# A Macaron block with a selective scan: the scan's gate copies issued one background part behind their products, in pinned order, with the Silu behind the last

## The chip, the cores and the metric

The kernel runs on one core of one Trainium2 chip. The time is device microseconds of one execution; the kernel before was run three times, with a median of 3204.71 us. In the lines of the profile PE is TensorE (matmuls), PEld its weight loads, DVE is VectorE, ACT is ScalarE, POOL is GpSimd and SP is SyncE, which issues nearly all DMAs here. All data is fp32.

## The reference

The input x has 4 sequences of 1024 rows of 512 columns. The block is half an FFN, a selective-scan (Mamba) layer, and half an FFN again:

```python
def ffn(x):                      # INTER = 1408
    g = einsum('th,ih->ti', x, gate_w) * gate_s
    u = einsum('th,ih->ti', x, up_w) * up_s
    return einsum('ti,hi->th', silu(g) * u, down_w) * down_s

def attn(x):                     # I = 1024, N = 16, K = 4, R = 128
    proj = einsum('blh,oh->bol', x, W_in)
    h, gate = split(proj, 2)                       # 1024 channels each
    h = silu(depthwise_conv(h, conv_w) + conv_b)
    ts, Bm, Cm = rms of the three parts of einsum('bil,oi->blo', h, Wx)
    delta = softplus(einsum('blr,ir->bil', ts, Wdt) + dt_bias)
    # per channel and per state n, along l:
    #   s = exp(delta * A) * s + delta * Bm * h ;  y += s * Cm
    y = (scan + D * h) * silu(gate)
    return einsum('bil,hi->blh', y, Wout)

x = x + 0.5 * ffn(layernorm(x))
x = x + attn(layernorm(x))
x = x + 0.5 * ffn(layernorm(x))
```

The change is about the `gate` half of `proj` and its Silu.

## The kernel before

The 4096 rows are cut into 16 stages of 256 rows (`k` = 0 to 15, four for each sequence). A stage scans its 256 rows; beside the scan it works through a list of background parts. The scan of a stage is 8 groups `i` of 128 channels with 4 units `g` each. A unit (`unit`, lines 557 to 596) makes four exponentials on ACT (L573, PSUM tiles `da`), two products on POOL (L578, tiles `sb`), four scans on DVE (L582) and two products with C on DVE (L592). A unit's sums over the states are small matmuls on PE (`yps`, L604), issued four units at a time one unit behind. PSUM has four tiles for `da`, and three (`ps_m`, banks 5, 6 and 7) that every other product shares: FFN products, the scan's gate products, the convolution's, the transposes.

The background of stage k (`background`, L717) is a list of parts made by hand: the FFN of other rows (11 parts `gate_w`, each a product and an eviction on ACT, L287; 11 parts `up_w`, evicted by DVE, L304; then `down_w`), and woven between them, two to an FFN part, the 8 parts of the scan's own gate (`gate`, L538), the two transposes of the next stage's rows (`tpm`, evicted on ACT, L238), the output projection of the stage before (`op`, L637, added by DVE, L645) and the convolution of the next stage (`hp`, L376, first tap on ACT, L380, three taps on DVE, L387). In stages 1 to 15 the order is: `gate_w` 0, 1, 2, then gate parts 0 and 1, `gate_w` 3, gate parts 2 and 3, `gate_w` 4, gate parts 4 and 5, `gate_w` 5, gate parts 6 and 7, `gate_w` 6, the two transposes, `gate_w` 7, the first half of `op`, `gate_w` 8, the second half, and so on. After `gate_w` 3, 7 and 10 a Silu over the evicted columns follows (`silu`, L197); it loads a table before it and after it. The number of FFN rows beside a stage (`BESIDE`, L39) is 512 in stages 2, 3, 5, 6, 8, 9, 11 and 12, which are called wide here, and 384 in the others, called narrow. Stage 0 has `up_w` parts in place of `gate_w` parts.

A gate part is four matmuls into a `ps_m` tile (`gp`, L545) and a copy of 128x256 to the resident tile `g_all` (L549). After the eighth copy Silu runs over all of `g_all` (2048 columns). `gated` (L614) multiplies the scan's result by it on POOL, from group 4 of the same stage on.

The main loop (L795) emits a unit and then as many parts as their cost allows. Two things set the order on an engine. A scheduler orders what was emitted, and may move an instruction if nothing ties it. `pin` (`keep_in_program_order`) ties an instruction behind the one that was emitted on its engine directly before it. And `defer(parts, f)` (L154) holds a piece of emission back until so many further parts with a cost have been emitted (`passed`, L158); `do` (L168) emits the part first and then what has come due. Before the change the gate copy is emitted with its own product, and is pinned in stage 0 alone.

Of the kernel before, what the change touches and what calls it, by code (L numbers as in the profile page):

```python
# [20 lines left out]
NI = I // P  # L21
NF = INTER // P
T = 256
# [19 lines left out]
def macaron_kernel(ctx: ExitStack, tc: tile.TileContext, a: dict, out: bass.AP):  # L43
    nc = tc.nc
# [37 lines left out]
    g_all = const.tile([P, NI, T], F32, name="g")  # L82
# [68 lines left out]
    pin = tc.keep_in_program_order  # L151
    deferred = []

    def defer(parts, emit):  # L154

        deferred.append([parts, emit])
# [33 lines left out]
    def cols(t):  # L190
        return t.rearrange("p (k o) -> p k o", k=KH)
# [5 lines left out]
    def silu(t):  # L197

        pin(nc.scalar.activation(t, t, AF.Silu))
        pin(nc.scalar.preload_act_table_set("natural_log_exp_and_others"))  # L200
# [42 lines left out]
    class FFN:  # L243
# [35 lines left out]
        def gate(self):  # L279
            self.done = 0  # L280

            def part(it):
                def emit(w):
                    if it == 0:
                        self.hd = p1.tile([P, NF, 2 * T], F32, tag="hd", name=f"hd{self.name}")
                    gp = self.product("gate_w", it, w[0])
                    nc.scalar.activation(  # L287
                        self.hd[:, it, : self.n], gp, AF.Copy, scale=gate_s[:, it : it + 1]
                    )
                    if it % 4 == 3 or it == NF - 1:  # L290
                        h = self.hd[:, self.done : it + 1, : self.n]
                        silu(h)
                        self.done = it + 1

                return Work(KH * self.n, 0, emit, [("gate_w", it)], settled=it == 0)

            return [part(it) for it in range(NF)]
# [240 lines left out]
    def gate(k):  # L538
        def part(i):
            def emit(w):  # L540
                assert k == 0 or ("gated", i) in st[k - 1]
                gp = ps_m.tile([P, 512], F32, tag="mm", name=f"gp{k}_{i}")
                w = cols(w[0])
                for kk in range(KH):
                    nc.tensor.matmul(  # L545
                        gp[:, :T], lhsT=w[:, kk, :], rhs=st[k]["xnT"][:, kk, K - 1 :],
                        start=(kk == 0), stop=(kk == KH - 1),
                    )
                (nc.scalar.copy if k else lambda *t: pin(nc.scalar.copy(*t)))(g_all[:, i, :], gp[:, :T])  # L549
                if i == NI - 1:  # L550
                    silu(g_all)

            return Work(KH * T, 0, emit, [("W_in", NI + i)])

        return [part(i) for i in range(NI)]
# [363 lines left out]
```

## Time and profile before

| what | value |
|---|---|
| three runs | 3203.93 to 3205.31 us, median 3204.71 us |
| the profiled execution | 3208.17 us, of which its span is 3206.3 us |
| granted TensorE clock, mean | 0.986 |
| gate copies L549 | 128, 47.5 us busy, 371 ns each |
| matmuls of the gate parts L545 | 1024, 388 ns each |
| table loads on ACT, L199, L200 and L573 | 86, 86 and 2, 1283 ns each |
| Silu of `g_all` | 16, 1912 ns each |
| exponentials L573 | 2048, 472 ns each |

The span runs from the first instruction to the last. The durations below come from this one execution. Its time is 3.5 us above the median of the runs.

Each row of a timeline gives start, duration, engine, line, operation, out<-in, shape, how many were merged, and in brackets how long the engine sat idle before it and what ended that.

### The profile page before, as it was taken

The page shows a single profiled execution, that of the slowest core. Times are in us where ns is not written, and L with a number is a line of the kernel's source. Part 1 is how long each engine was busy: PE and PEld are TensorE (multiplying, and loading weights), DVE is VectorE, ACT ScalarE, POOL GpSimd, SP SyncE. Part 2 cuts the span into 40 slices and gives each one's busy share as a digit, 9 for nine tenths or more (in the row PEclk, how much of TensorE's full clock was granted, in tenths as well). Part 3 has the DMA queues.
Part 4 walks back from the last instruction along what each step waited for, and adds up shares of the span by engine and source line. Part 5 has one row for each costly group of instructions (what it writes and reads, how often), then busy time and mean ns, then how long its engine had stood idle before and what let it go on. Part 6 is the DMA issues. An engine that isn't in the chain of part 4 may idle for free.

```text
span 3206.3 us, 41927 instructions
## 1 busy us (share of the span) xinstructions
PE 3059.7 (95%) x12448; PEld 1644.7 (51%) x12448; DVE 2477.8 (77%) x4981; ACT 1780.1 (56%) x3531; POOL 1938.5 (60%) x1895
## 2 busy tenths in 40 slices
PE   8988899999999999999999999999999999899999
PEld 3554454545555454545545454554555455454434
DVE  1259788888869887887988788798878779798931
ACT  3265555747465664646565474656557475656530
POOL 0066758566766766666675756667575667658610
PEclk9999999999999999999999999999999999999999
DMA  5364566556566655645665654656565564566531
GB/s 171 113 174 119 158 188 171 161 137 184 134 174 181 178 161 148 184 123 160 191 178 159 164 164 123 183 165 171 168 178 161 140 186 132 170 183 178 169 94 43
DMA packets 287427, 506.43 MB, mean 158 GB/s; under 512 B 32097, under 2 KB 50273, under 8 KB 287201
## 3 DMA queue, kind: packets, MB, share of 16 engines
q1 hardware_dynamic: 285616, 503.31, 55.8%
q8 instruction: 100, 1.64, 0.2%
q14 instruction: 127, 1.03, 0.1%
q10 hardware_dynamic: 1584, 0.45, 0.1%
HBM read 442.03 MB, written 61.60 MB: 157 GB/s over the span
## 4 chain that ended last, share of the span: by engine, by line
PE 63%; DVE 21%; ACT 6%; POOL 5%; issue 5%; DMA 1%; DVEq 0%; SPq 0%; POOLq 0%; ACTq 0%
DVE da L582 12%; PE fo L319 12%; PE gate_w L273 12%; PE up_w L273 9%; PE hp L376 5%; PE op L637 5%; PE gp L545 5%; PE yps L604 5%; DVE sb L592 4%; POOL sb L578 3%; ACT da L573 2%; PE gate_wp L273 1%; PE gate_we L273 1%; PE dp L490 1%; PE foe L319 1%
## 5 line engine op out<-in xcount | busy, mean ns | idle before, releaser
L578 POOL TENSOR_TENSOR sb<-rep,bc 128x512 f32<-128x512 f32 x1024 | 1279.4, 1275 | 421.3 <-PE yps L604 302.8
L582 DVE TENSOR_TENSOR_SCAN da<-da,state,sb 128x256 f32<-128x256 f32 x1536 | 1059.7, 740 | 250.9 <-ACT da L573 215.6
L573 ACT ACTIVATE da<-rep,a_w 128x256 f32<-128x256 f32 x2048 | 899.5, 472 | 508.9 <-DVE sb L592 488.0
L592 DVE TENSOR_TENSOR sb<-da,bc 128x512 f32<-128x512 f32 x1024 | 688.8, 680 | 1.7 <-issue 0.4
L273 PE MATMUL gate_w<-fxT,w_gate_w 128*128 128x384 f32 (+1 forms) x1408 | 564.2, 547 | 8.6 <-ACT hd L287 6.3
L273 PE MATMUL up_w<-fxT,w_up_w 128*128 128x384 f32 (+1 forms) x1408 | 557.8, 546 | 3.0 <-DVE hd L304 2.4
L319 PE MATMUL fo<-w_down_w,hd 128*128 128x512 f32 x1232 | 549.4, 599 | 0.0
L273 PEld LDWEIGHTS gate_w<-fxT,w_gate_w 128*128 128x128 f32 x1408 | 268.1, 193 | 256.2 <-issue 154.9
L604 PE MATMUL yps<-sb,fold 128*32 128x256 f32 x4096 | 332.0, 389 | 62.8 <-DVE sb L592 54.1
L273 PEld LDWEIGHTS up_w<-fxT,w_up_w 128*128 128x128 f32 x1408 | 260.7, 190 | 254.1 <-issue 150.8
L582 DVE TENSOR_TENSOR_SCAN da<-da,sb 128x256 f32<-128x256 f32 x512 | 322.6, 679 | 78.6 <-ACT da L573 62.2
L319 PEld LDWEIGHTS fo<-w_down_w,hd 128*128 128x128 f32 x1232 | 230.1, 192 | 273.0 <-issue 271.5
L521 POOL TENSOR_SCALAR e<-z 128x512 f32<-128x512 f32 x64 | 124.4, 1944 | 237.3 <-ACT z L502 223.1
L604 PEld LDWEIGHTS yps<-sb,fold 128*32 128x32 f32 x4096 | 127.7, 110 | 271.4 <-DVE sb L592 122.9
L376 PE MATMUL hp<-mxT,w_W_in 128*128 128x259 f32 x1024 | 244.3, 386 | 23.1 <-issue 12.4
L545 PE MATMUL gp<-mxT,w_W_in 128*128 128x256 f32 x1024 | 244.7, 388 | 4.0 <-ACT dd L499 3.3
L376 PEld LDWEIGHTS hp<-mxT,w_W_in 128*128 128x128 f32 x1024 | 192.5, 191 | 83.5 <-issue 30.4
L637 PE MATMUL op<-w_Wout,u 128*128 128x512 f32 x512 | 228.1, 595 | 0.3 <-POOL u L616 0.3
L545 PEld LDWEIGHTS gp<-mxT,w_W_in 128*128 128x128 f32 x1024 | 195.4, 193 | 63.0 <-issue 19.8
L387 DVE SCALAR_TENSOR_TENSOR u<-hp,conv_w,u 128x256 f32<-128x256 f32 x384 | 178.0, 473 | 14.7 <-ACT u L380 12.2
L287 ACT ACTIVATE hd<-gate_w,gate_s 128x384 f32<-128x384 f32 (+1 forms) x176 | 110.5, 629 | 130.4 <-PE gate_w L273 129.6
L304 DVE SCALAR_TENSOR_TENSOR hd<-up_w,up_s,hd 128x384 f32<-128x384 f32 (+1 forms) x176 | 118.2, 672 | 69.0 <-PE up_w L273 68.9
(112 smaller groups left out, 2649.9 us busy)
## 6 DMA issues: line engine op xcount, KB each, us to landing
rep<-row SPq DMA_DIRECT2D x512, 256.0 KB, 4.9
w_W_in<-in_W_in_dram SPq DMA_DIRECT2D x256, 256.0 KB, 3.6
w_gate_w<-in_gate_w_dram SPq DMA_DIRECT2D x198, 256.0 KB, 4.0
w_up_w<-in_up_w_dram SPq DMA_DIRECT2D x198, 256.0 KB, 4.1
w_down_w<-down_w SPq DMA_DIRECT2D x187, 256.0 KB, 2.7
row<-dd SPq DMA_DIRECT2D x128, 256.0 KB, 3.4
w_Wout<-in_Wout_dram SPq DMA_DIRECT2D x128, 256.0 KB, 4.6
bc<-bcd SPq DMA_DIRECT2D x64, 256.0 KB, 4.9
```

The source lines that it names most:

```text
L273: nc.tensor.matmul(o[:, : self.n], lhsT=w[:, k, :], rhs=self.xT[:, k, : self.n], start=(k == 0), stop=(k == KH - 1),)
L319: nc.tensor.matmul(op, lhsT=self.hd[:, it, t * P : (t + 1) * P], rhs=wd[it], start=(it == 0), stop=(it == NF - 1),)
L376: nc.tensor.matmul(hp[:, : K - 1 + T], lhsT=w[:, kk, :], rhs=st[k]["xnT"][:, kk, :], start=(kk == 0), stop=(kk == KH - 1),)
L387: pin(nc.vector.scalar_tensor_tensor(u[:, i, :], hp[:, q : q + T], conv_w[:, i, q : q + 1], u[:, i, :], ALU.mult, ALU.add,))
L521: lambda: pin(nc.gpsimd.tensor_scalar(e, z, 1.0, 1.0, ALU.add, ALU.subtract)),
L545: nc.tensor.matmul(gp[:, :T], lhsT=w[:, kk, :], rhs=st[k]["xnT"][:, kk, K - 1 :], start=(kk == 0), stop=(kk == KH - 1),)
L573: e = nc.scalar.activation(da[:, j, :], rep[:, h + j, 0, :], AF.Exp, scale=a_w[:, b0 + h + j, g : g + 1])
L578: nc.gpsimd.tensor_tensor(sb, rep[:, hs, 1, :], d["bc"][:, g : g + 1, :].to_broadcast([P, 2, T]), ALU.mult)
L582: nc.vector.tensor_tensor_scan(da[:, j, :], da[:, j, :], sb[:, j, :], 0.0 if first else state[:, b0 + h + j, g : g + 1], ALU.mult, ALU.add,)
L592: nc.vector.tensor_tensor(sb, da, d["bc"][:, NS + g : NS + g + 1, :].to_broadcast([P, 2, T]), ALU.mult)
L604: nc.tensor.matmul(yp[j * Q : (j + 1) * Q, :], lhsT=fold, rhs=pr[j // 2][:, j % 2, :], start=(g == 0), stop=(g == NS - 1),)
L637: nc.tensor.matmul(op, lhsT=st[k]["u"][:, i, j * P : (j + 1) * P], rhs=wo[i], start=(i == 0), stop=(i == NI - 1),)
```

## The change

Product and copy of a gate part are separated. The copy is put off by one part with a cost, and every copy is pinned, in all stages. The Silu is emitted right behind the eighth copy, as before, so it is put off with it.

```diff
                         gp[:, :T], lhsT=w[:, kk, :], rhs=st[k]["xnT"][:, kk, K - 1 :],
                         start=(kk == 0), stop=(kk == KH - 1),
                     )
-                (nc.scalar.copy if k else lambda *t: pin(nc.scalar.copy(*t)))(g_all[:, i, :], gp[:, :T])
-                if i == NI - 1:
-                    silu(g_all)
+
+                def out_of():
+                    pin(nc.scalar.copy(g_all[:, i, :], gp[:, :T]))
+                    if i == NI - 1:
+                        silu(g_all)
+
+                defer(1, out_of)
 
             return Work(KH * T, 0, emit, [("W_in", NI + i)])
```

The functions that it calls:

```python
    def defer(parts, emit):
        deferred.append([parts, emit])

    def passed(entries):
        for e in entries:
            e[0] -= 1
        while deferred and deferred[0][0] <= 0:
            deferred.pop(0)[1]()

    def silu(t):
        pin(nc.scalar.activation(t, t, AF.Silu))
        pin(nc.scalar.preload_act_table_set("natural_log_exp_and_others"))
```

Built, the changed program has the same instructions as before on PE, DVE, POOL and SP, and one table load more on ACT. SP's order is the same throughout. On ACT, in a wide stage (stage 3), the part of the order that differs reads as follows (c0 to c7 are the gate copies, e3 is the eviction of `gate_w` 3, S a Silu with its two table loads, t0 and t1 the evictions of the two transposes, x4 four exponentials):

```
before  c0 c1 e3 S c2 x4 c3 x3 e4 x c4 x4 c5 x .. x2 e5 c6 c7 S(g) e6 t0 x8 e7 x S t1 x7
after   c0 e3 S c1 x4 c2 x3 e4 c3 x c4 x5 .. x2 e5 c5 c6 e6 c7 S(g) t0 x4 e7 x S t1 x8
```

In a narrow stage (stage 4):

```
before  c0 x2 c1 e3 S c2 c3 x5 e4 x3 c4 x3 c5 x .. e5 x c6 x3 c7 S(g) e6 t0 e7 S x4 t1 x8
after   c0 x2 e3 S c1 x4 c2 e4 c3 x4 c4 x4 .. e5 c5 x2 c6 x2 e6 c7 S(g) t0 e7 S x4 t1 x8
```

The three `ps_m` banks are also dealt out in another order. In stage 3, for example: `gate_w` 4 takes the bank of gate product 1 (before: that of `gate_w` 3), gate product 5 that of `gate_w` 4 (before: that of gate product 3), gate product 7 that of `gate_w` 5 (before: that of the `dp` product), the second transpose that of `gate_w` 6 (before: that of gate product 7), and `gate_w` 7 that of gate product 7 (before: that of `gate_w` 6).

## The prediction

> **What bounds the kernel now.** First the page's busy times and the chain of waits.
>
> ```profile
> PE 3059.7 (95%) x12448; PEld 1644.7 (51%) x12448; DVE 2477.8 (77%) x4981; ACT 1780.1 (56%) x3531; POOL 1938.5 (60%) x1895
> ...
> PE 63%; DVE 21%; ACT 6%; POOL 5%; issue 5%; DMA 1%; DVEq 0%; SPq 0%; POOLq 0%; ACTq 0%
> ```
>
> PE leads, with 146.6 us idle in all, and DVE holds a fifth of the chain. So any gain has to come out of those 146.6 us. Next, windows: length, then busy time of PE, PEld, DVE, ACT and POOL. The first is the gate part of stage 3 (wide), the last that of stage 4 (narrow).
>
> ```profile
> 732.50:765.80 33.30, 33.30 (x173) 21.47 (x171) 25.17 (x42) 26.40 (x47) 22.55 (x25) 1.00 0.77 217
> 800.50:860.00 59.50, 58.15 (x265) 30.98 (x265) 52.96 (x97) 30.40 (x68) 37.38 (x41) 1.00 0.51 136
> 916.20:951.20 35.00, 31.39 (x173) 21.54 (x171) 27.02 (x59) 26.53 (x49) 27.11 (x28) 1.00 0.74 209
> ```
>
> In a wide stage PE has no idle moment while the gate is computed: there is nothing to win there, and a PE wait that appears is lost. In a narrow stage PE idles 3.6 us. Third, the table of waits (total, times, longest):
>
> ```profile
> DVE da L582 <- ACT da L573: 277.8, 88, 11.2
> ACT g L549 <- PE gp L545: 49.5, 36, 5.2
> ```
>
> DVE starves when exponentials come late, and ACT spends 49.5 us standing at a gate copy whose product isn't ready, with exponentials queued behind. That is the most the change could take off ACT. Fourth, the timeline of ACT in stage 3 around Silu of `g_all`, and DVE beside it:
>
> ```profile
> 759.75 0.37 ACT L549 COPY g<-gp 128x256 f32<-128x256 f32 x1 [0.81 <-PE gp L545]
> 760.14 1.28 ACT L199 ACT_TABLE_LOAD   x1
> 761.43 1.91 ACT L199 ACTIVATE g<-g 128x2048 f32<-128x2048 f32 x1
> 763.36 1.28 ACT L200 ACT_TABLE_LOAD   x1
> 764.66 0.69 ACT L287 ACTIVATE hd<-gate_w,gate_s 128x512 f32<-128x512 f32 x1
> 765.24 0.58 ACT L238 COPY mxT<-tpm 128x512 f32<-128x512 f32 x1
> 765.71 3.27 ACT L573 ACTIVATE da<-rep,a_w 128x256 f32<-128x256 f32 x8
> ```
> ```profile
> 767.09 2.68 DVE L582 TENSOR_TENSOR_SCAN da<-da,state,sb 128x256 f32<-128x256 f32 x4 [4.06 <-ACT da L573]
> ...
> 776.46 0.76 DVE L582 TENSOR_TENSOR_SCAN da<-da,state,sb 128x256 f32<-128x256 f32 x1 [1.21 <-ACT da L573]
> ```
>
> The 4.5 us of the Silu with its two loads (760.14 to 764.64) run while PE makes `gate_w` 6 (759.55 to 762.98). That is the overlap the change touches.
>
> **The change part by part, wide stages (8).** I walk stage 3. (a) Copy 1 now stands behind eviction 3 and a Silu, and ends at 745.2, where copy 2 ended (744.81 + 0.37); `gate_w` 4 needs that bank and started at 744.91: PE waits 0.3. Gate product 5 now needs eviction 4, which ended at 751.37; PE is there at 750.4 (748.34 + 1.73 + 0.3): 1.0 more. The second transpose needs eviction 6, about 0.35 behind the first: PE is 1.7 late at `gate_w` 7. (b) Silu of `g_all` now starts behind eviction 6 and copy 7. `gate_w` 6 ends at 762.98 + 1.4 = 764.4; eviction 0.69, copy 0.37, Silu block 4.50 and transpose eviction 0.58 bring the next exponentials to 770.5 instead of 765.71: 4.8 us. Queued behind are t0 and x4, and DVE waits for the latter: its scans start at 771.9 instead of 767.09. (c) Then the Silu of `gate_w` 4 to 7 comes, and before it only 5 exponentials instead of 9 now stand. DVE works off its one unit in 4.0 us (to 775.9) and waits again: eviction 7, one exponential, the block and t1 end at 778.4, scans go on near 778.8. The unit that started at 776.46 starts one unit later, near 783: DVE is 6.5 late. (d) A DVE wait of 1.2 for `op` (at 786.72) takes 1.2 back: 5.3. (e) What PE feels of it:
>
> ```profile
> 802.52 0.76 DVE L582 TENSOR_TENSOR_SCAN da<-da,state,sb 128x256 f32<-128x256 f32 x1 [1.95 <-POOL sb L578]
> 803.74 0.76 DVE L582 TENSOR_TENSOR_SCAN da<-da,state,sb 128x256 f32<-128x256 f32 x1 [0.46 <-POOL sb L578]
> ```
> ```profile
> 796.89 3.67 PE L376 MATMUL hp<-mxT,w_W_in 128*128 128x259 f32 x16
> ```
>
> The first product's taps (L387, four groups of 0.46 to 1.65 us from 793.64) free a bank near 795.9, which convolution product 2 wants at 796.89: 1.0 of slack. In the changed order a scan and a product (1.4 us) move behind these taps. So PE starts that product 5.3 - 1.4 - 1.0 = 2.9 late. On DVE's side the waits of 1.95 and 0.46 for POOL swallow 2.4 of the 5.3, which leaves 2.9 as well. Behind this both engines are nearly full (58.15 and 52.96 of 59.5 us), so 2.9 stays. Stage 2 by the same steps: scans 580.46 to 585.25, 6.3 late at the third unit, no wait for `op`, slack 1.5, hence 3.4 on PE; POOL waits of 2.66 leave 3.6 on DVE: 3.5. Stages 5, 8, 11 look like 2, and 6, 9, 12 like 3. Sum: 4 x 3.5 + 4 x 2.9 = 25.6 us.
>
> A bound below: DVE's lateness hidden wholly, PE's own 1.65 a stage, 13 us. Above: none hidden, 4 x 6.3 + 4 x 5.3 = 46 us. I take 25.6, since each deduction has a row.
>
> The price of a table set. [...] Here the load row is 1.28 and Silu starts 0.01 behind its end. [...]
>
> **Narrow stages.** In stage 4:
>
> ```profile
> 927.10 0.37 ACT L549 COPY g<-gp 128x256 f32<-128x256 f32 x1
> 930.67 0.37 ACT L549 COPY g<-gp 128x256 f32<-128x256 f32 x1 [3.20 <-PE gp L545]
> 930.94 2.07 ACT L573 ACTIVATE da<-rep,a_w 128x256 f32<-128x256 f32 x5
> ```
>
> Copy 3 waits 3.2 us for a product that PE can't begin before DVE has fed it, and five exponentials stand behind. Now x4 come right behind copy 1, at 927.4: 3.5 us earlier. Most is given back: eviction 4 waits for PE's 932.99 in both orders, with the next exponentials behind, so DVE's lead shrinks to 1.2. Later `gate_w` 7 loses its wait of 1.53 for eviction 6 (it needs copy 7 now, 947.9 + 0.37), but `op` then waits for t0, at 953.35 against 953.92, and the exponentials behind the next Silu come at 958.0 against 958.81. I book 0.7 a stage for 4, 7, 10 and 13. In stages 1 and 14 the corresponding step is 406.65 against 408.06: 1.4 each. Together -5.6 us.
>
> **At nothing.** Stages 0 and 15: the order moves by a few exponentials, and DVE's or PE's other waits end there last; 2 us either way. The copies themselves: same 128 of 371 ns on an engine 56% busy. Table loads: two single extra ones vanish (stages 1, 14) and three appear (4, 7, 15): 1.28 us of ACT, behind four fresh exponentials that give DVE 4 us of work. PE and POOL: a few `yps` matmuls of 0.06 us and the 12-column edge copies (0.2 us) change places. SP issues the same DMAs in the same order, and none waits on `g_all`; `gated` reads it two groups later.
>
> Sum: 25.6 - 5.6 = +20 us: span 3226.3 from 3206.3, the profiled execution 3228.2 from 3208.17, the median 3224.7 from 3204.71. I say 3225.
>
> **Rivals.** What differs by less than 0.2% (6.4 us) can't be told from no change.
> 1. Only PE's waits count (15%): DVE's later idle (3.8 us from 804 to 857) swallows its lateness. 13.2 - 5.6 = +7.6: 3212. Against it: the taps and the bank of `hp`.
> 2. None is hidden (13%): DVE's lateness reaches the next stage. 46 - 5.6: 3246. Against it: the waits for POOL and `op` that are there to take it.
> 3. Faster (12%): the place is the exponentials behind the Silu of `gate_w` 0 to 3 in the seven narrow stages; freed from copies 2 to 4 they start 3.5 us earlier, and if PE's idle time there shrinks by as much that is 24.5 us, against 13.2 lost in wide ones: 3193. It decides once a narrow stage keeps over 1.9 us. For it: 9.88 us of DVE idle in stage 1 before such exponentials. Against it: eviction 4.
> 4. No change (8%): the scheduler's new order fits the waits, 3205.
>
> Mine has 52%. Slower: 52 + 13 and two thirds of rival 1, 75%. Within: 13%. Faster: 12%. The range, 3203 to 3246, leaves out rival 3 and the upper half of rival 2.
>
> **What would show it.** Right: in wide stages the wait of DVE's scans for `da` behind Silu of `g_all` grows from 4 to 9 us, and a second one near 3 appears; PE idles before convolution product 2 for `hp`'s taps; wide stages 3 us longer, narrow ones about 1 shorter; the 49.5 us at the copies mostly gone. Wrong: PE full in the wide stages' gate part and their length unchanged, or narrow stages 2 us shorter.

## The result, and the profile after

The changed kernel takes 3223.94 us (median of 4 runs, 3223.79 to 3224.88); before takes 3204.32 (4 runs, 3203.93 to 3205.31). The ratio is 1.0061, with a 95% interval of 1.0048 to 1.0074: slower by 0.6%, or 19.6 us. The two profiled executions differ by less: a span of 3222.3 us against 3206.3, 16.0 more. The profile after lies at its kernel's median (3224.07 us), the one before 3.5 us above (3208.17).

Where the 16.0 lie is read from the first gate product (L545) of each stage, which stands at the same place in both kernels; a stage's length runs from one to the next. Differences to before, in us:

| stages | forecast | measured | by stage |
|---|---|---|---|
| wide, 2 3 5 6 8 9 11 12 | +25.6 | +23.6 | 3.4 2.5 3.3 3.8 1.3 3.8 3.8 1.8 |
| narrow, 1 4 7 10 13 14 | -5.6 | -13.2 | -5.1 -0.8 -0.5 -1.5 -2.6 -2.6 |
| 0 | 0 | +2.3 | |
| 15, with the end | 0 | +3.6 | |
| ahead of stage 0 | 0 | -0.4 | |

3.3 of these microseconds belong to the profile of before and not to the change. PE's granted clock falls to 0.50 now and then, for 3.4 us or a multiple of it (more on this at the end). The last experiment but one (How much slack) adds a copy to the kernel before in the wide stages alone, and in its stages 1 and 13 ACT and PE have the same order as before. Yet these two stages are 1.6 and 1.7 shorter, and each lacks one such stretch of 3.4 us. Around the start of stage 13, before and then with the added copy (length, busy time of PE, PEld, DVE, ACT and POOL, granted clock, DMA share, GB/s):

```profile
2569.80:2590.00 20.20, 18.54 (x88) 12.46 (x87) 13.58 (x28) 12.19 (x23) 18.22 (x16) 0.92 0.84 250
```
```profile
2580.90:2601.10 20.20, 18.53 (x96) 12.78 (x95) 15.23 (x32) 13.48 (x26) 18.20 (x16) 1.00 0.88 263
```

Without these two stretches the narrow stages gained 9.9 and not 13.2, and the sum is +19.3, close to the 19.6 of the medians. Every stage difference in this document is taken against this one profile of before, so where a kernel lacks both stretches, the same 3.3 is in its figure for the narrow stages.

The page's busy times and chain of waits, for the changed kernel:

```profile
PE 3068.8 (95%) x12448; PEld 1637.0 (51%) x12448; DVE 2475.5 (77%) x4981; ACT 1779.6 (55%) x3532; POOL 1936.9 (60%) x1895
...
PE 53%; DVE 24%; ACT 10%; issue 6%; POOL 6%; DMA 2%; SPq 0%; ACTq 0%; DVEq 0%; POOLq 0%
```

Apart from one table load on ACT the instructions are the same; what changed is who waits for whom. Ten points of the chain left PE, and ACT's share rose from 6 to 10%. The table of waits (total, times, longest) says the same:

```profile
DVE da L586 <- ACT da L577: 295.1, 88, 11.3
...
ACT hd L287 <- PE gate_w L273: 192.9, 75, 8.8
```

DVE waits 17 us more for exponentials. ACT's wait at the gate copies is down from 49.5 to 11.4, but its wait at the FFN evictions is up from 129.6 to 192.9. Together that is 179.1 before and 204.3 now: ACT's wait for PE moved to another instruction and grew.

Stage 3, which the prediction walked through, begins 0.13 us later than before, so its times can be laid side by side. The chain of waits within it (start, length, what), first of before, then of the changed kernel:

```profile
759.71 3.43 PE gate_w L273 x8
763.14 0.87 PE tpm L235 x8
...
765.88 3.63 PE gate_w L273 x8
```
```profile
761.27 3.45 PE gate_w L273 x8
...
764.74 0.69 ACT hd L287
...
767.00 1.91 ACT g L199
...
770.81 1.57 ACT da L577 x4
...
774.66 1.91 ACT hd L199
...
778.93 0.77 DVE da L586
```

Before, the chain stays on PE from the gate products to convolution product 2; the Silu of `g_all` is not in it. Now it leaves PE twice: from 736.28 to 751.52, where the bank waits told of below stand, and again at the end of `gate_w` 6. There it passes eviction 6, Silu of `g_all`, four exponentials and the next Silu, and goes on over DVE's scans. DVE's side:

```profile
772.08 2.68 DVE L586 TENSOR_TENSOR_SCAN da<-da,state,sb 128x256 f32<-128x256 f32 x4 [8.93 <-POOL dd L510]
...
778.93 1.55 DVE L586 TENSOR_TENSOR_SCAN da<-da,state,sb 128x256 f32<-128x256 f32 x2 [3.00 <-ACT da L577]
```

The first wait is put down to POOL, but the exponentials began at 770.70 and the scans 1.38 later, as before: it is the exponentials that came last. The wait of 4.06 became 8.93. The one of 3.00 stands a unit earlier than the 1.21 of before, which is gone. On PE two small waits stand in the gate part (0.16 before `gate_w` 4, for copy 1; 0.74 in gate product 5, for eviction 4; both are shown with the first experiment), and this one before convolution product 2, which stood at 796.89:

```profile
800.18 3.75 PE L376 MATMUL hp<-mxT,w_W_in 128*128 128x259 f32 x16 [0.88 <-ACT da L577]
```

The row names an exponential on ACT, which ended 0.26 before. A tap on DVE ended 0.10 before (at 800.08), which fits a release better (PE's longer waits end 0.05 to 0.06 behind, in the median) and is the wait that the prediction named. That tap is one of this group of four, which started at 794.61 before:

```profile
798.82 1.65 DVE L387 SCALAR_TENSOR_TENSOR u<-hp,conv_w,u 128x256 f32<-128x256 f32 x4
```

### The profile page after: what moved, and what is told of

It reads as the page before. It is cut to its first block, busy times and chain, and to the rows that moved or that the text cites. A ratio compares the mean times of both kernels' runs of the same rounds, so it can differ in the third digit from the quotient of the medians.

```text
span 3222.3 us, 41899 instructions
## 1 busy us (share of the span) xinstructions
PE 3068.8 (95%) x12448; PEld 1637.0 (51%) x12448; DVE 2475.5 (77%) x4981; ACT 1779.6 (55%) x3532; POOL 1936.9 (60%) x1895
## 4 chain that ended last, share of the span: by engine, by line
PE 53%; DVE 24%; ACT 10%; issue 6%; POOL 6%; DMA 2%; SPq 0%; ACTq 0%; DVEq 0%; POOLq 0%
DVE da L586 15%; PE fo L319 11%; PE up_w L273 9%; PE gate_w L273 8%; DVE sb L596 5%; PE hp L376 5%; PE yps L608 4%; PE gp L545 3%; ACT da L577 3%; POOL sb L582 3%; PE op L641 2%; PE gate_we L273 1%; PE gate_wp L273 1%; ACT hd L199 1%; PE foe L319 1%
## 5 line engine op out<-in xcount | busy, mean ns | idle before, releaser
L545 PE MATMUL gp<-mxT,w_W_in 128*128 128x256 f32 x1024 | 242.4, 385 | 14.4 <-ACT dd L499 7.3
L545 PEld LDWEIGHTS gp<-mxT,w_W_in 128*128 128x128 f32 x1024 | 191.0, 190 | 76.9 <-issue 20.9
L287 ACT ACTIVATE hd<-gate_w,gate_s 128x384 f32<-128x384 f32 (+1 forms) x176 | 110.1, 626 | 193.7 <-PE gate_w L273 192.9
```

The costliest lines, as they stand in the source:

```text
L545: nc.tensor.matmul(gp[:, :T], lhsT=w[:, kk, :], rhs=st[k]["xnT"][:, kk, K - 1 :], start=(kk == 0), stop=(kk == KH - 1),)
```

## The experiments

Spans of single executions of one kernel scatter by 1 to 7 us, and the kernel before had medians of 3206.53, 3205.07 and 3205.23 us in the three sets of runs. Each time below is compared with its own set; differences of stages are taken between single profiles.

**Which half of the change costs: copies or Silu.** First the copies alone:

```diff
-                defer(1, out_of)
+                if i >= NI - 2:
+                    out_of()
+                else:
+                    defer(1, out_of)
```

> Copies 0 to 5 one part behind and pinned; copies 6 and 7 and Silu of g_all with their products, as before. Theory (two causes add up in a wide stage: PE's waits for banks behind copy 1 and eviction 4, and the late Silu): only PE's 1.3 to 1.4 us a wide stage remain, 8 x 1.4 = +11, the narrow stages keep most of their gain, -8 to -10, stages 0 and 15 cost 2 to 5; time 3205 to 3211. Rival A (all the loss of wide stages is the late Silu): the wide stages cost nothing, time near 3195. Rival B (all of it is the copies' banks): wide +23.6 stays, time near 3220.

Measured: 3208.74 against 3206.53, ratio 1.0007 (0.9998 to 1.0016). Wide stages +6.9, narrow -10.9, stage 0 +1.3, stage 15 +3.4. PE's row in stage 3 has both bank waits and no third one:

```profile
744.90 3.70 PE L273 MATMUL gate_w<-fxT,w_gate_w 128*128 128x512 f32 x8 [0.16 <-ACT g L551]
...
751.08 2.00 PE L545 MATMUL gp<-mxT,w_W_in 128*128 128x256 f32 x8 [0.75 <-ACT hd L287]
```

The time is in the expected range, and stage 3 is 1.4 longer, as expected of banks alone. Then the last copy and the Silu alone:

```diff
-                defer(1, out_of)
+                if i == NI - 1:
+                    defer(1, out_of)
+                else:
+                    (nc.scalar.copy if k else lambda *t: pin(nc.scalar.copy(*t)))(g_all[:, i, :], gp[:, :T])
```

> Copies 0 to 6 as before; only copy 7 and Silu of g_all one part behind. Theory: exponentials behind the Silu 3.3 us late (769.0 for 765.7 in stage 3), a second DVE wait near 3, DVE 5 late at the third unit, of which 1.2 (op) and 2.4 (order, slack, POOL) are swallowed: 1.4 a wide stage, +11, narrow stages -1 to 0 each; time 3212 to 3216. Rival A (all the loss is the late Silu): +24, 3228. Rival B (all of it is the copies' banks): 3204.

Measured: 3218.42 against 3206.53, ratio 1.0041 (1.0028 to 1.0053). Wide +12.0, narrow -3.1, stage 15 +4.9. The time is 2.4 above the expected range, far below rival A's 3228 and far above rival B's 3204. DVE and PE in stage 3:

```profile
770.75 2.68 DVE L589 TENSOR_TENSOR_SCAN da<-da,state,sb 128x256 f32<-128x256 f32 x4 [7.49 <-ACT da L580]
777.61 1.55 DVE L589 TENSOR_TENSOR_SCAN da<-da,state,sb 128x256 f32<-128x256 f32 x2 [3.00 <-ACT da L580]
```
```profile
798.85 3.75 PE L376 MATMUL hp<-mxT,w_W_in 128*128 128x259 f32 x16 [0.88 <-ACT da L580]
```

The late Silu alone brings both DVE waits and PE's wait before convolution product 2, but not the two bank waits in the gate part; PE comes 0.7 late at `gate_w` 7, behind the second transpose. The two halves together make 6.9 + 12.0 = 18.9. Stages 6 and 9 hold a stretch of PE at half clock in some profiles and not in others: the next two kernels leave the wide stages as they were, and yet the first lacks the stretch in stage 6, the second in stage 9, and each is 1.7 shorter there. Of the two halves, the one with the copies lacks it in both stages, the one with the Silu in stage 9. With 1.7 added back for each, the halves make 24.0. That is the 23.6 of the change: both causes are real, and in the wide stages they add up.

**Only the narrow stages.**

```diff
+                if sum(BESIDE[k]) == 3 and 0 < k < NCS - 1:
+                    defer(1, out_of)
+                else: (copy and Silu with the product, as before)
```

> The change in stages 1, 4, 7, 10, 13, 14 alone; all others as before. The stage lengths of the changed kernel (-5.1, -0.8, -0.5, -1.5, -2.6, -2.6) taken as they stand: -13.1, time 3191. Stage 1's contains 2.3 that stage 0 had lost and gives back: -10.8, time 3193.5. The prediction's terms: -5.6, 3198.7. Rival (the narrow stages were shorter only because the wide ones ahead had been late): 3204.

Measured: 3195.67 against 3206.53, ratio 0.9968 (0.9956 to 0.9980); span 3191.9, narrow stages -11.5. By the medians that is 10.9 less: the 3193.5 that was worked out is 10.8 below before, the prediction's terms 5.6, the rival nothing. The gains are the narrow stages' own, and the wide ones lose by themselves.

**Is it the deferral at all?** The change also pins the copies, which the kernel before did in stage 0 alone. Pinned, but not deferred:

```diff
-                (nc.scalar.copy if k else lambda *t: pin(nc.scalar.copy(*t)))(g_all[:, i, :], gp[:, :T])
+                pin(nc.scalar.copy(g_all[:, i, :], gp[:, :T]))
```

> The copies pinned, none deferred. The order on ScalarE is that of before in the wide stages; in stage 4 four exponentials instead of five change sides with copies 2 and 3. Theory: within 2 us of before, 3202 to 3206. Rival (the pins do the harm): over 3210.

The kernel is faster, and neither expectation foresaw it: 3195.01 against 3206.53, ratio 0.9964 (0.9952 to 0.9977). Narrow stages -15.7, more than with the change; wide ones with no new wait; stage 15 +3.4. ACT in stage 4 shows how:

```profile
920.51 0.37 ACT L549 COPY g<-gp 128x256 f32<-128x256 f32 x1
920.77 1.67 ACT L573 ACTIVATE da<-rep,a_w 128x256 f32<-128x256 f32 x4
924.08 0.37 ACT L549 COPY g<-gp 128x256 f32<-128x256 f32 x1 [1.63 <-PE gp L545]
```

Without the pin copy 3 stood ahead of five exponentials and waited 3.20 us; with it four of them go first. The first line below is DVE before, the second DVE with all copies pinned, at the same scans of stage 4:

```profile
932.31 2.44 DVE L582 TENSOR_TENSOR_SCAN da<-da,sb 128x256 f32<-128x256 f32 x4 [4.34 <-ACT da L573]
```
```profile
922.15 2.44 DVE L582 TENSOR_TENSOR_SCAN da<-da,sb 128x256 f32<-128x256 f32 x4 [0.77 <-ACT da L573]
```

The counterpart, deferred but not pinned:

```diff
-                    pin(nc.scalar.copy(g_all[:, i, :], gp[:, :T]))
+                    nc.scalar.copy(g_all[:, i, :], gp[:, :T])
```

> All eight copies deferred as in the change, but not pinned; Silu and its load back pinned. The order on ScalarE falls back nearly to that of before in the narrow stages (copies 2 and 3 ahead of five exponentials), and in wide stages Silu of g_all stands ahead of eviction 6 again. Theory (deferral costs where it holds Silu and banks up, the gain sits at copies 2 and 3): within 5 us of before. Rival (deferral as such costs): near the changed kernel, +15 or more.

Measured: 3205.86 against 3205.07, ratio 1.0001 (0.9992 to 1.0010). The scheduler undoes most of the deferral of a copy that isn't pinned: in stage 4 all eight copies stand as before, and in stage 3 it is copies 2 and 3 that stand elsewhere, behind four exponentials. The even total is a balance, though. In the profile narrow stages are 9.5 shorter (6.2 without the stretches in stages 1 and 13), wide ones 2.3 longer and stage 0 3.2 longer, where this kernel also lacks the pins that before has. In the narrow stages eviction 6 now stands ahead of the table load behind the Silu; whether that is their gain was not tested. So the loss in the wide stages is deferral held by pins, and the narrow stages can have a gain without deferral. The next two runs ask which pins.

```diff
+                ((lambda *t: pin(nc.scalar.copy(*t))) if k < NCS - 1 else nc.scalar.copy)(...)
```

> Copies pinned in stages 0 to 14, none deferred, stage 15 as before. Theory: the profile of all pinned had -15.4 with +3.4 of it in stage 15, so 3.4 less: span 3187.5, 18 to 19 below before (0.994). Rival (stage 15's 3.4 is work that only changes sides of the stage's border): as all pinned, 15 below before.

Measured: 3191.53 against 3205.07, ratio 0.9959 (0.9945 to 0.9972); stage 15 at +0.5 instead of +3.4. The time is 13.5 below before, not the 18 to 19 expected; the span of 3188.6 is near the expected 3187.5, which had been worked out from the long profile of before. Pinned in all stages the kernel was 11.5 below, and the two intervals overlap, so the gain of this step is seen in the profile of stage 15 alone. With all pinned, PE stands 0.67, 0.73 and 1.46 us in stage 15 before `dp`, a gate product and `gate_w` 5, for ACT (an eviction L287, a gate copy L549 and L499), where before has no such wait; that is most of the 3.4.

```diff
+                ((lambda *t: pin(nc.scalar.copy(*t))) if k == 0 or (i in (2, 3)
+                    and k < NCS - 1 and sum(BESIDE[k]) == 3) else nc.scalar.copy)(...)
```

> Only copies 2 and 3 pinned, in stages 1, 4, 7, 10, 13 and 14, nothing deferred. In 4, 7, 10 and 13 the order is that of all pinned. Theory (the gain of the narrow stages sits at the four exponentials that stand ahead of copy 3): 4, 7, 10 and 13 as short as with all pinned, -1 to -3 each; in 1 and 14 a later part of the order stays as before and half of their -5.3 and -3.2 is kept; span 3193 to 3197. Rival (the gain comes from the pins of the other copies): 3204 or more.

A single run: 3200.13 against a median of 3205.23, span 3198.2, just above the expected range. Stages 4 and 7 are as short as with all pinned (-1.8, -1.0), 10 and 13 half as much or less (-0.8, -1.2 of -1.6, -3.0), and 1 and 14 keep little (-1.6, 0.0) of -5.3 and -3.2. Stage 13 has the stretch of before here and lacks it with all pinned, so its -1.2 is nearly all of the -1.3 that are left there; the -1.6 of stage 1 is the stretch that before has there. So copies 2 and 3 carry the gain in 4, 7 and 13, in this one run; the rest comes from the order behind them.

**How much slack stood behind the Silu.** One copy of `g_all` onto itself, 1.90 us of ACT, ahead of its Silu in the wide stages, in the kernel before and in the changed one:

```diff
                 if i == NI - 1:
+                    if sum(BESIDE[k]) == 4:
+                        pin(nc.scalar.copy(g_all, g_all))
                     silu(g_all)
```

> Before, with one more ScalarE copy of g_all onto itself (2048 columns, about 1.9 us) in front of Silu of g_all in the eight wide stages. Theory (before has slack behind that Silu: exponentials 1.9 late, the next Silu 1.4 late, of which the wait for op takes 1.2): 0 to 0.3 a wide stage, +0 to +3 in all. Rival (every microsecond of ScalarE there is on the path): +1.9 each, +15.

> The changed kernel with the same extra copy of g_all in the eight wide stages. Theory (the slack is used up by the change: op, the order, hp's bank and POOL): the whole 1.9 shows in each wide stage, +12 to +15 over the changed kernel. Rival (DVE's later idle swallows it, only PE's bank waits count): +0 to +4.

Both missed, on a single run each. Before: 3218.05 against 3205.07, 13.0 more and so nearer to the rival's 15; in the profile the wide stages are 9.1 longer. Changed: 3232.64 against 3223.94, +8.7 instead of 12 to 15. There stages 2, 3, 5, 8 and 12 are 1.3 to 2.2 longer, 11 is the same, and 6 and 9 are 1.9 shorter, as each lacks its stretch at half clock. In before, stage 3, the cause is on PE, where the forecast had reckoned with DVE alone:

```profile
766.97 3.70 PE L273 MATMUL gate_w<-fxT,w_gate_w 128*128 128x512 f32 x8 [1.45 <-ACT hd L287]
```

Eviction 6 stands behind Silu of `g_all` there and holds the bank of `gate_w` 7. Its end at 765.35 left 0.46 us to 765.81, so 1.9 more cost PE 1.45. DVE came out as expected: its second wait stayed 1.21. The order before was thus near a limit of its own, on a different engine. Which step swallows the 1.9 in stages 6, 9 and 11 of the changed kernel stays open.

**One Silu block fewer.** On top of pins to stage 14, Silu of `g_all` beside another Silu in the narrow stages, sharing its table loads:

```diff
+                        if it == 7 and beside_gate.get(self.name):      # or NF - 1
+                            pin(nc.scalar.activation(g_all, g_all, AF.Silu))
                         silu(h)
```

> Copies pinned in stages 0 to 14; in stages 1, 4, 7, 10, 13, 14 Silu of g_all stands directly ahead of the Silu of gate_w 4 to 7 and shares its table loads: 2.6 us less ScalarE a stage, a block of 1.9 us longer ahead of the next exponentials. Theory (what counts is when the exponentials behind the block come): 1 to 2 us later each, 3196 to 3204. Rival (the loads saved count): 2.6 each less, 3176.

> As the one before, but Silu of g_all beside the Silu of gate_w 8 to 10, where it shares the loads too. Theory: the block behind copy 7 is gone, the exponentials and evictions behind it come up to 4.5 us earlier, PE's wait for eviction 6 and DVE's for the exponentials shrink: 0.5 to 2 a stage, 3180 to 3188. Rival (the exponentials wait for gate_w 7 in any order, and 1.9 us come later): 3191 to 3198.

Measured: 3210.36 and 3215.99 against 3205.23, ratios 1.0014 (1.0005 to 1.0024) and 1.0029 (1.0020 to 1.0039). Both lose to the pins alone, the first by more than expected, the second against expectation. In the second, stage 1 is 193.5 us instead of 180.1; PE has a wait of 3.23 for DVE's addition of `op` and one of 7.73 for DVE's copy of the turned parameters (L459), where it had 2.03. PE stands there at half clock for 27.3 us instead of 10.2, which is 8.6 of lost clock. Why DVE comes so late stays open.

## Why the prediction was right, and where not

**The verdict and the time.** 3225 was forecast and 3223.94 measured; slower had 75%. The sum was +20 and came out as 19.6 in the medians, +16.0 in the pair of profiles and +19.3 without the two stretches in the profile of before. That it is so close is partly luck. By the profiles the wide stages cost 2.0 less than forecast and the narrow ones gained 4.3 more, and stages 0 and 15, put at nothing, cost 5.9.

**Wide stages: right in mechanism and size.** (a) The bank waits: forecast 0.3 and 1.0, so 1.3 behind gate product 5; measured 0.31 and 1.12 (together 1.43: `gate_w` 5 at 754.22 for 752.66, less 0.13). At `gate_w` 7 it is 2.1 instead of 1.7, since two of the `yps` matmuls went between the two transposes. Copies only shows these waits by themselves. (b) Exponentials 770.70 for a forecast 770.5, scans 772.08 for 771.9. (c) The second wait is 3.00, and scans go on at 778.93 for 778.8. (d) and (e): convolution product 2 is 3.2 late for 2.9, the stage 2.5 longer. Stage 2: 3.4 for 3.5. The classes were less even than assumed: stages 8 and 12 lose 1.3 and 1.8, 6 and 9 lose 3.8. Rival 1 (only PE's waits count) falls by the run with the last copy and the Silu alone: +12.0 in the wide stages without the two bank waits, where PE's own lateness at `gate_w` 7 is 0.7 in stage 3. Rival 2 (nothing hidden) falls by the 23.6, where it had 46.

**Narrow stages: the term that was mis-sized.** "I book 0.7 a stage for 4, 7, 10 and 13" and "1.4 each" for 1 and 14 made -5.6; the table has -13.2, of which 3.3 belong to the profile of before. The rest, -9.9, is 4.3 more than forecast. Stages 4, 7 and 13 fit (-0.8, -0.5, -0.9); 1 gains 2.1 too much, 14 1.2 and 10 0.8. In stage 1 the working left out PE's clock. PE before, in stage 1, with the window around it (length, busy time of PE, PEld, DVE, ACT, POOL, then the granted clock):

```profile
387.36 0.83 PE L604 MATMUL yps<-sb,fold 128*32 128x256 f32 x2 [3.23 <-DVE u L611]
389.13 3.78 PE L545 MATMUL gp<-mxT,w_W_in 128*128 128x256 f32 x8 [0.94 <-ACT dd L499]
392.70 3.62 PE L273 MATMUL gate_w<-fxT,w_gate_w 128*128 128x384 f32 x8
```
```profile
382.20:399.70 17.50, 12.29 (x58) 7.73 (x56) 11.22 (x27) 13.12 (x23) 8.87 (x12) 0.80 0.08 30
```

The same stretch of the changed kernel:

```profile
382.50:398.30 15.80, 12.46 (x74) 7.80 (x73) 14.63 (x32) 11.64 (x23) 8.03 (x12) 1.00 0.46 114
```

Behind its gaps PE ran at half clock for 6.8 us, and eight gate matmuls took 3.78 instead of 1.89, eight of `gate_w` 3.62 instead of 2.74: 2.8 us beyond the gap itself. The changed kernel has a gap of 3.34 at the same place and no loss of clock. Over the six narrow stages PE stood 51 us at half clock before (44 without the two stretches in stages 1 and 13), 34 with the change and 31 with pins alone; half of such time is lost clock. Stage 1 lost 10.2 of clock before (8.5 without its stretch) and 3.4 with the change, stage 10 6.8 and 3.4. There the clock can be the reason for what the forecast missed, but how much of it lay on the path is not separated. In stage 14 it is not the reason: 1.7 were lost in both. Why that stage gained 1.2 more stays open. The prediction's own sign of being wrong, narrow stages 2 us shorter, was met by stages 1 and 14 (-3.5 and -2.6); the mean of the six is -1.65.

Rival 3 (faster) had the right place, and its condition, over 1.9 us kept in a narrow stage, was met in the same two stages; the wide stages' loss outweighed it.

**What carried the narrow gain.** The prediction credited it to the deferral. The runs show that pins alone bring 15.7 in the profile (12.4 without the two stretches), more than pins with deferral, and that deferral without pins leaves the time as it was. No rival foresaw this: the pin was read as a part of the deferral, and not as an edit with a price of its own.

**At nothing.** Stage 0 was 2.3 longer and stage 15 3.6, where 2 either way was allowed. In stage 15 pins alone cost as much (+3.4, and +0.5 with none there). They are not the only thing that can cost there: with only the last copy put off and pinned it was +4.9, with 5.1 more of lost clock than before. In stage 0 the product of `hp` at 251 takes 6.51 us instead of 5.40 behind a gap of 5.9 that both kernels have: a part of it is again the clock (17.1 lost in the stage instead of 15.4).

**The table loads.** They came out as the row says: in stage 3 of the changed kernel the load takes 1.28 us, from 765.70, and Silu of `g_all` starts at 767.00, 0.02 behind its end.

## What to carry to other kernels

Pinning an instruction and deferring it are two edits: run each alone before judging both, because a scheduler may have been putting exactly the waiting instruction first. Taking ScalarE's wait away at the gate copies (49.5 us before, 11.4 after) moved it to the FFN evictions (129.6 before, 192.9 after), which wait for the same engine. It paid where work that was ready got in front, and cost where a long block (here a Silu with two table loads, 4.50 us) lost the matmul it was hidden behind. Before pushing anything behind such a block, list what holds PE's banks there, on both sides of the change. And before reading stage by stage, see how far the profiled execution lies from the median: here one profile was 3.5 us long.

## What the runs showed of the hardware

The granted clock of PE has two values here, 1.00 and 0.50. But for the one at the very end of a profile, the stretches at 0.50 last 3.41 us or a multiple of it: in the profile of before there are 18, in that of the changed kernel 13, of 3.41, 6.83 or 10.24 us each. A stretch cost up to 1.7 us: that is what stages 6, 9 and 13 differ by in profiles with the same order.

The length of a gap alone does not decide whether the clock falls. In stage 1 a gap of 1.93 us (all copies pinned, from 383.25) was followed by 3.4 us at 0.50, gaps of 3.23 and 0.94 (before) by 6.8, and one of 3.34 (changed) by none. Two stretches of 3.41 us each, of before and of all copies pinned (up to the fall of the clock, and from it on) and of the changed kernel (around its gap); the first number behind the length is PE's busy time:

```profile
384.21:387.62 3.41, 0.26 (x2) 0.14 (x2) 3.41 (x8) 2.81 (x6) 1.11 (x4) 1.00 0.30 113
387.62:391.03 3.41, 2.47 (x7) 1.55 (x6) 3.10 (x7) 3.41 (x9) 0.00 (x0) 0.50 0.00 0
```
```profile
383.07:386.48 3.41, 1.48 (x7) 1.17 (x7) 3.41 (x9) 3.41 (x9) 0.00 (x0) 1.00 0.35 129
386.48:389.89 3.41, 3.41 (x8) 2.13 (x7) 3.33 (x7) 3.31 (x7) 2.09 (x3) 0.50 0.00 0
```
```profile
383.38:386.79 3.41, 1.89 (x6) 0.76 (x4) 3.41 (x9) 2.15 (x4) 2.13 (x6) 1.00 0.28 79
386.79:390.21 3.42, 1.60 (x7) 1.43 (x8) 3.42 (x9) 3.42 (x9) 0.00 (x0) 1.00 0.13 49
```

Ahead of the two falls PE was busy for 0.26 and 1.48 of the 3.41 us. In the changed kernel it was busy for 1.89 and 1.60 in the two stretches around its gap, and the clock stayed at 1.00. What decides the fall of the clock these three cases do not show.

The same order can have a stretch at 0.50 in one execution and none in another. Stage 9 has one before, from 1964.58, behind 3.41 us in which PE was busy for 1.36, and is 186.7 us long at a mean clock of 0.99; with all copies pinned it has none and is 185.0 long at 1.00. Stage 13 has one before, from 2582.39, behind 3.41 us with 1.75 of work on PE; with the added copy the clock is 1.00 there, and the stage 1.7 shorter.
